# A clear of a small unused tile on GpSimd behind every gather from a table in HBM

## The chip, the core and the metric

The kernel runs on one core of a Trainium2 chip. The metric is the device time of one execution in microseconds (us): the median of several runs. A core has five engines that each work through an instruction stream of their own: TensorE (PE in the profile), VectorE (DVE), ScalarE (ACT), GpSimd (POOL) and SyncE (SP). They wait for one another by semaphores only. DMA transfers are issued by SP, ACT or POOL and run beside the engines.

## What is computed

One message-passing layer of a graph network, with a residual and a layer norm. There are 12,500 nodes with 128 features (x) and 400,000 edges, sorted by destination, each with a length. Cut to what matters, with the constants left out:

```python
rbf = exp(-(d[:, None] - centers) ** 2 / (2 * width ** 2))          # 50 per edge
cut = 0.5 * (cos(pi * d / 10) + 1) * (d <= 10)
W = (silu(rbf @ fw1 + fb1) @ fw2 + fb2) * cut[:, None]              # 128 per edge
messages = (x[src] @ pw + pb) * W
agg = segment_sum(messages, dst, 12500)
out = layernorm(2 * x + silu(agg @ mw1 + mb1) @ mw2 + mb2)
```

Edges longer than 10 contribute nothing. The kernel drops them first and works on those that are left.

## The kernel before

**Tiles and stages.** The edges that are left are handled in 139 quads (`NL`) of 512 edges: four groups of 128, one edge to a partition. Instead of multiplying each gathered row of x by `pw`, the kernel multiplies all 12,500 rows once in the first 60 us or so (`project`) and stores the products in HBM as the table of products, `proj`. From there on a quad needs only its rows of `proj`. For the first 12 quads (`FROM_X`), which come before that table is there, rows of x are gathered and multiplied afterwards (`multiply`, line 983).

**One quad.** `radial` loads the lengths, `basis` makes the radial functions (ACT), `first`, `silu` and `second` are the two layers that give W (PE, ACT, PE). `message` (line 1103) multiplies W with the gathered rows on DVE at line 1110; `place` (line 1117) makes one-hot matrices on DVE at line 1122, which hold the destination and the cutoff; `sum_up` (line 1134) multiplies messages and one-hot matrices on PE, and `add` (line 1161) adds the sums into the node table `aggT` on DVE. Node layers and layer norms of finished nodes are worked in between (`nodes`) and the last of them at the end (`tail` and the lines behind the loop).

**Packing.** Which edges are left, in which order, is worked out on the chip in seven chunks (`pack_first`, `pack`, `unpack`), mostly on DVE. Each chunk sends its list to HBM with one indirect DMA from POOL (line 487) and reads it back; that gives the indices `srci` (line 891) by which rows are gathered.

**The gathers.** `fetch` (line 1026) issues one indirect DMA on POOL for each group of 128 edges: 128 rows of 512 bytes, to one quarter of a buffer. In the first 12 quads the table is x; from quad 12 on it is `proj`. In eight quads (`SINGLY`) the first group is not gathered but loaded row by row from SP (`one_by_one`). That makes 48 gathers from x and 500 from `proj`. The rare branches behind the main path (`more`, `everything`), which these inputs don't take, call `fetch` with an `idx` of their own.

**What sets the order.** The schedule is written out by hand (`tc.manual_schedule()`): each engine executes its instructions in the order in which the Python code emits them. `fetches` (line 435) decides when a gather is emitted. It keeps a model of POOL's time, `pool[0]`, which grows by 1.29 us with each gather, and emits gathers up to a given time or quad. POOL's own stream holds nothing but the gathers of line 1032, the seven scatters of line 487 and a few small instructions in the first 5 us, so on POOL their order is fixed, and the model decides only how the seven scatters stand among the gathers, and how the instructions of other engines stand to each other. Buffers (`quad_sb`, 21 of them) come free when the message that used them is done; a gather into a used buffer waits for that. POOL has no other work.

Of the kernel before, what the change touches and what calls it, by code (L numbers as in the profile page):

```python
# [10 lines left out]
F32 = mybir.dt.float32  # L11
# [9 lines left out]
P = 128  # L21
# [5 lines left out]
WIDE_0 = 128  # L27
WIDTHS = (56, 56, 80, 112, 80, 104, 128)
QT = 4
QE = QT * P  # L30
WS = 500
SB = 14
# [48 lines left out]
def kernel(  # L81
# [37 lines left out]
    nc = tc.nc  # L119
# [4 lines left out]
    NP = 2 * NQ  # L124
    MW = 2 * (NQ * QE + QE)

    CLEAR = (0, 128 * P, 384 * P, MW)
    assert H == P == W and DIRECT % QT == 0 and LISTS <= 5
    assert E == P * sum(ROWS) and E % P == 0 and W <= N <= 1 << SB
# [4 lines left out]
    keep = ctx.enter_context(tc.tile_pool(name="keep", bufs=1))  # L134
# [54 lines left out]
    make_identity(nc, ident)  # L189
    quad_sb = [keep.tile([P, QT, H], F32, name=f"quad{k}") for k in range(GOT)]  # L190
    x4_sb = [keep.tile([P, QT, H], F32, name=f"x4{k}") for k in range(X_BUFS)]
    quad_sb += x4_sb
# [62 lines left out]

    ones_b = keep.tile([96, QE], BF16, name="ones_b")
    nc.vector.memset(ones_b, 1.0)
# [34 lines left out]
    def ends():  # L292


        nc.vector.tensor_scalar(end, part_f, 2.0, float(2 * NQ * QE - FIRST_W),
                                op0=OP.mult, op1=OP.add)
# [108 lines left out]
    def place_of(q):  # L405
        n, later = LATER
        while len(placed) <= q:
            k = len(placed)
            last = {}
            for m, b in enumerate(placed):  # L410
                last[b] = m
            allowed = range(len(quad_sb)) if k < n else later
            cap = max(4, min(20, 20 - (k - 30) // 4))
            ok = [b for b in allowed if last.get(b, -99) <= k - cap]
            never = [b for b in allowed if b not in last]
            if k < len(quad_sb):
                placed.append(k)
            elif ok:
                placed.append(max(ok, key=lambda b: last.get(b, -99)))
            else:  # L420
                placed.append(min(allowed, key=lambda b: last.get(b, -99)))
        return placed[q]
# [12 lines left out]
    def fetches(until, most):  # L435

        while fetched[0] < QT * min(most, known[0]) and pool[0] <= until:
            q, j = divmod(fetched[0], QT)
            fetch(q, table=x if q < FROM_X else None, js=(j,))
            if j == 0:  # L440
                pool[0] = max(pool[0], summed.get(before_it(q), 0.0))
            if j or q not in SINGLY:
                pool[0] += 1.29
            there_at[q] = pool[0] + 2.2
            fetched[0] += 1
# [349 lines left out]
    def unpack(c):  # L795
# [8 lines left out]
        def listed(t, a, b, l0, l1):  # L804
            (nc.scalar if c < 1 else nc.sync).dma_start(t[a:b, :l1 - l0],
                              packed[l0:l1, (p0 + a) * 512:(p0 + b) * 512]
                              .rearrange("s (p w) -> p s w", w=512))
# [3 lines left out]
        if c < 2:  # L811
            more_ = np_ if c == 0 else SPILL
            also = work.tile([P, 2, QE], F32, name="s", bufs=3).bitcast(I32)
            listed(also, 0, more_, 3, LISTS)
# [194 lines left out]
    def one_by_one():  # L1009

        row_at[0] = max(row_at[0], clock[0] - 8.0)
        while singles and row_at[0] < clock[0]:
# [4 lines left out]
            if e % AT_ONCE == 0:  # L1017
# [5 lines left out]
                              proj.rearrange("n f -> (n f)").bitcast(U8)[ds(rows_at[e % AT_ONCE], 4 * H)]  # L1023
                              .rearrange("(o f) -> o f", o=1))

    def fetch(q, idx=None, table=None, js=range(QT)):
        got = quad_sb[place_of(q) if q >= 0 else 0]
        for j in js:
            if q in SINGLY and j == 0:
                continue  # L1030
            i = srci[:, 2 * q + j // 2, j % 2:j % 2 + 1] if idx is None else idx[:, j:j + 1]
            nc.gpsimd.indirect_dma_start(  # L1032
                out=got[:, j, :], out_offset=None, in_=proj if table is None else table,
                in_offset=bass.IndirectOffsetOnAxis(ap=i, axis=0))
        got_of[q] = got

    def quads(o):
# [3 lines left out]
    def radial(o, lengths):  # L1041

        n = math.prod(lengths.shape) // QE
        d = work.tile([P, QE], F32, name="d", bufs=3)
        v = lengths.rearrange("(o h) e -> o h e", o=1)
# [494 lines left out]
    def more(q):  # L1540

        fetch(-2, srci[:, 2 * q:2 * q + 2, :].rearrange("p r j -> p (r j)"))
        radial(-1, near_d[2 * q:2 * q + 2].rearrange("(o p) e -> o (p e)", o=1))
        basis(-1)
        first(-1)
        silu(-1)
        second(-2)
        pu_of[q], got_of[q] = pu_of.pop(-2), got_of.pop(-2)
        place(q)
        msg = message(q)  # L1550
        pa_of["two"] = ps.tile([P, 2, 2 * W], F32, name="sums", bufs=2)
        sum_up(q, msg)
        base_of(q)
        add(q)

    def everything():
        nc.vector.memset(aggT, 0.0)
        def again(e0, seen):
# [18 lines left out]
            cosine(wgt)  # L1577
            nc.vector.scalar_tensor_tensor(wgt, wgt, 1.0, near, op0=OP.add, op1=OP.mult)
            fetch(-2, idx)
            radial(-1, edge_weight[ds(e0, QE)].rearrange("(o e) -> o e", o=1))  # L1580
            basis(-1)
# [65 lines left out]
```

## Time and profile before

| | |
|---|---|
| time, median of 3 runs | 727.36 us (726.96 to 729.21) |
| time of the profiled execution | 731.18 us |
| its span, first to last instruction | 729.3 us |
| mean granted TensorE clock | 0.926 |
| gathers from `proj` (line 1032) | 421 into `quad` buffers, 79 into `x` buffers |
| gathers from x (line 1032) | 48 |
| scatters (line 487) | 7 |

How to read the profile: a row of the groups has the line, the engine, the operation, output and inputs by name, and a count; then the busy time in us and the mean of one in ns; then the idle time of the engine just ahead of these instructions and what ended it. A row of the timeline begins with the start and the length in us and ends, in brackets, with the idle time ahead. "issue" is idle time that ended by nothing that the profile shows. A row of the waits has the total in us, the number of waits and the longest. In the rows of one line's summary stand the shortest, median and longest duration in ns and the first and last start. POOLq and DVEq are the sequencers of POOL and DVE.

### The profile page before, as it was taken

Reading aid. Unit: us, or ns where it says so; the run is one execution under the profiler, and the core shown is the slowest. Engines: PE = TensorE matmul, PEld = TensorE weight load, DVE = VectorE, ACT = ScalarE, POOL = GpSimd, SP = SyncE. Lnnn points to the kernel's source line nnn. Section 1 sums busy time; section 2 is a strip of 40 time slices with the busy share of each in tenths; the row PEclk is TensorE's granted clock in tenths of the full one; section 3 lists DMA queues with packets and bytes.
Section 4 is the critical chain, followed back from the end, with each engine's and each line's share of the span. In section 5 each row is a group of like instructions: output and inputs, shape, how many; then the busy total and the mean of one; then the engine's idle time right before and its main releaser. Section 6 shows DMA issues by size and latency. Waiting matters only on the chain.

```text
span 729.3 us, 13631 instructions
## 1 busy us (share of the span) xinstructions
PE 591.7 (81%) x3531; PEld 463.5 (64%) x3531; DVE 561.8 (77%) x1734; ACT 402.7 (55%) x572; POOL 532.4 (73%) x569
## 2 busy tenths in 40 slices
PE   6878777797888797888788979999977878887974
PEld 5767566576656676667466757777755656565752
DVE  8897998878968998989689959768555546564774
ACT  6547634275345864536347364839644744374584
POOL 6776777777777777777777777777777777777770
PEclk9998887999989998999889998999998989999998
DMA  8995443243234333242333343434433433445242
GB/s 262 326 314 182 124 134 87 68 145 90 87 100 140 86 96 106 84 141 81 88 99 121 104 105 114 147 116 142 126 99 113 139 99 98 112 125 149 55 139 69
DMA packets 53104, 91.38 MB, mean 125 GB/s; under 512 B 13824, under 2 KB 20576, under 8 KB 53018
## 3 DMA queue, kind: packets, MB, share of 16 engines
q1 hardware_dynamic: 34610, 53.34, 22.0%
q0 software_dynamic: 17840, 36.77, 19.6%
q8 instruction: 30, 0.49, 0.3%
q14 instruction: 56, 0.46, 0.2%
q10 hardware_dynamic: 568, 0.33, 0.2%
HBM read 74.59 MB, written 15.79 MB: 124 GB/s over the span
## 4 chain that ended last, share of the span: by engine, by line
DVE 25%; POOL 18%; PE 17%; issue 16%; DMA 15%; ACT 4%; DVEq 2%; SPq 1%; POOLq 0%; ACTq 0%
POOL quad L1032 14%; DMA quad<-proj,srci 7%; POOL x L1032 5%; DVE hot L1122 4%; PE bank L1099 4%; PE sums L1142 4%; PE ph L1082 3%; DVE aggT L1165 2%; DVE msg L1110 2%; PE bank L327 2%; DMA pair<-packed 2%; DVEq L1151 2%; DMA proj<-hp 2%; DVE r_d L502 2%; DVE quad L1122 2%
## 5 line engine op out<-in xcount | busy, mean ns | idle before, releaser
L1032 POOL DMA_INDIRECT quad<-proj,srci x421 | 400.5, 951 | 130.5 <-issue 104.9
L1099 PEld LDWEIGHTS bank<-fw_sb,s 128*128 128x128 f32 x1112 | 162.2, 210 | 67.5 <-issue 60.0
L1088 ACT ACTIVATE s<-ph 128x1024 f32<-128x1024 f32 x70 | 71.2, 1017 | 169.9 <-PE ph L1082 169.8
L1099 PE MATMUL bank<-fw_sb,s 128*128 128x128 f32 x1112 | 162.1, 293 | 0.0
L1082 PE MATMUL ph<-rbf,w_sb 102*128 102x512 f32 x278 | 141.1, 632 | 9.2 <-ACT rbf L1074 4.9
L1142 PEld LDWEIGHTS sums<-hot,msg 128*128 128x128 f32 x816 | 106.4, 196 | 55.2 <-DVE msg L1110 27.1
L1122 DVE TENSOR_SCALAR hot<-iota_n,dl,cut 128x80 f32<-128x80 f32 (+4 forms) x408 | 108.7, 343 | 24.8 <-PE sums L1142 22.0
L1142 PE MATMUL sums<-hot,msg 128*128 128x80 f32 (+4 forms) x816 | 109.5, 278 | 14.2 <-DVE msg L1110 13.9
L1096 PE MATMUL bank<-fb_b,ones_b 96*128 96x512 bf16 x139 | 56.8, 409 | 49.0 <-DVE msg L1110 24.5
L1032 POOL DMA_INDIRECT x<-proj,srci x79 | 75.3, 953 | 24.1 <-issue 20.7
L1110 DVE TENSOR_TENSOR msg<-bank,quad 128x512 f32<-128x512 f32 (+1 forms) x82 | 55.4, 676 | 41.6 <-DMA quad<-proj,srci 30.8
L1082 PEld LDWEIGHTS ph<-rbf,w_sb 102*128 102x128 f32 x278 | 50.5, 202 | 47.4 <-issue 36.7
L1165 DVE TENSOR_TENSOR aggT<-aggT,sums 128x80 f32 (+4 forms) x209 | 53.7, 257 | 27.4 <-PE sums L1142 10.7
L1073 ACT ACTIVATE rbf<-d,rbf_bias,rbf_scale 102x512 f32<-102x512 f32 x70 | 56.2, 803 | 26.5 <-DMA d<-near_d 26.4
L1032 POOL DMA_INDIRECT quad<-in_x_dram,srci x48 | 47.0, 979 | 18.7 <-issue 14.7
L327 PEld LDWEIGHTS bank<-pw_sb,xT 128*128 128x128 f32 (+1 forms) x292 | 43.5, 215 | 11.3 <-ACT xT L968 5.0
L1088 ACT ACT_TABLE_LOAD x36 | 46.2, 1283 | 0.6
L1074 ACT ACT_TABLE_LOAD x35 | 44.9, 1283 | 0.6
L327 PE MATMUL bank<-pw_sb,xT 128*128 128x128 f32 (+1 forms) x292 | 44.5, 301 | 0.8 <-ACT xT L968 0.6
L1074 ACT ACTIVATE rbf<-rbf 102x512 f32<-102x512 f32 x70 | 44.1, 630 | 1.5
L1142 PE MATMUL sums<-quad,quad 128*128 128x128 f32 (+3 forms) x296 | 42.4, 290 | 2.2 <-DVE quad L1110 1.9
L1110 DVE TENSOR_TENSOR quad<-bank,quad 128x512 f32<-128x512 f32 (+2 forms) x40 | 25.1, 631 | 24.3 <-DMA quad<-proj,srci 20.4
(268 smaller groups left out, 809.9 us busy)
## 6 DMA issues: line engine op xcount, KB each, us to landing
d<-near_d SPq DMA_DIRECT2D x70, 256.0 KB
dl<-proj SPq DMA_DIRECT2D x1024, 0.5 KB
x<-in_x_dram SPq DMA_DIRECT2D x46, 256.0 KB
quad<-proj,srci POOLq DMA_INDIRECT x421
proj<-hp SPq DMA_DIRECT2D x24, 256.0 KB
out_dram<-x SPq DMA_DIRECT2D x22, 256.0 KB
r_d<-in_edge_weight_dram SPq DMA_DIRECT2D x5, 256.0 KB
r_dst<-in_dst_dram SPq DMA_DIRECT2D x5, 256.0 KB
```

The lines of the kernel that those rows point to most:

```text
L327: nc.tensor.matmul(to[:m, k, :], lT[:, k * P:k * P + m], w, start=False, stop=(k == a + c - 1))
L1032: nc.gpsimd.indirect_dma_start(out=got[:, j, :], out_offset=None, in_=proj if table is None else table, in_offset=bass.IndirectOffsetOnAxi ...
L1073: nc.scalar.activation(rbf[:u], d[:u], AF.Square, bias=rbf_bias[:u], scale=rbf_scale[:u])
L1074: nc.scalar.activation(rbf[:u], rbf[:u], AF.Exp, scale=-1.0 / (2.0 * width * width))
L1082: nc.tensor.matmul(ph[:, h, :], w1_sb[:2 * KR, h, :], rbf[:2 * KR], start=True, stop=True)
L1088: nc.scalar.activation(s[:, :n], ph[:, :n], AF.Silu)
L1096: nc.tensor.matmul(pu, ones_b[:, :P], bias_b["fb2"].rearrange("k j f -> k (j f)"), start=True, stop=False)
L1099: nc.tensor.matmul(pu[:, j * H:(j + 1) * H], s[:, j * P:(j + 1) * P], fw2_sb, start=False, stop=(j == QT - 1))
L1110: nc.vector.tensor_mul(msg[:, a:b, :], pu_of[q].rearrange("p (j f) -> p j f", j=QT)[:, a:b, :], got_of[q][:, a:b, :])
L1122: nc.vector.tensor_scalar(hot[:, j, :wide(q)], iota_n[:, :wide(q)], dl[:, at[0], at[1]], cut[:, at[0], at[1]], op0=OP.is_equal, op1=OP.mult)
L1142: nc.tensor.matmul(pa[:, k * W:k * W + wide(q)], msg[:, j, :], hot[:, j, :wide(q)], start=(j % n == 0), stop=(j % n == n - 1))
L1165: nc.vector.tensor_add(to, to, pa[:, k * W:k * W + wide(q)])
```

## The change

A tile `pause` of 128 partitions by 128 float32 is added. Behind each gather from `proj` on the main path, GpSimd sets it to zero. No instruction reads the tile. The gathers from x and those of the rare branches get no clear. The model of POOL's time in `fetches` stays as it was.

```diff
@@ -27,6 +27,7 @@
 QT = 4
+PAUSE = 128
 QE = QT * P
@@ -1023,6 +1024,8 @@
+    pause = keep.tile([P, PAUSE], F32, name="pause")
+
     def fetch(q, idx=None, table=None, js=range(QT)):
         got = quad_sb[place_of(q) if q >= 0 else 0]
         for j in js:
@@ -1032,6 +1035,8 @@
             nc.gpsimd.indirect_dma_start(
                 out=got[:, j, :], out_offset=None, in_=proj if table is None else table,
                 in_offset=bass.IndirectOffsetOnAxis(ap=i, axis=0))
+            if table is None and idx is None:
+                nc.gpsimd.memset(pause, 0.0)
         got_of[q] = got
```

## The prediction

> **What bounds the kernel now.** I read the page first: the busy shares, the slices, the groups.
>
> ```profile
> span 729.3 us, 13631 instructions
> PE 591.7 (81%) x3531; PEld 463.5 (64%) x3531; DVE 561.8 (77%) x1734; ACT 402.7 (55%) x572; POOL 532.4 (73%) x569
> POOL 6776777777777777777777777777777777777770
> L1032 POOL DMA_INDIRECT quad<-proj,srci x421 | 400.5, 951 | 130.5 <-issue 104.9
> L1032 POOL DMA_INDIRECT x<-proj,srci x79 | 75.3, 953 | 24.1 <-issue 20.7
> L1032 POOL DMA_INDIRECT quad<-in_x_dram,srci x48 | 47.0, 979 | 18.7 <-issue 14.7
> ```
>
> By busy share PE and DVE look more loaded than POOL. The slices say otherwise: POOL stands at 7 from the second slice to the last but one, and never varies. An engine with slack would show dips. The groups say what the missing three tenths are: 421 + 79 = 500 gathers from the table of products have 130.5 + 24.1 = 154.6 us of idle time ahead of them, 0.31 us each, most of it put down to "issue", that is, to no other engine. Next I read POOL's timeline, a piece from the middle and the end, and the one line's own summary.
>
> ```profile
> 73.87 0.94 POOL L1032 DMA_INDIRECT quad<-proj,srci  x1 [0.30 <-issue]
> ...
> 299.66 0.94 POOL L1032 DMA_INDIRECT quad<-proj,srci  x1 [0.30 <-issue]
> 300.91 0.94 POOL L1032 DMA_INDIRECT quad<-proj,srci  x1 [0.30 <-issue]
> 302.16 0.99 POOL L1032 DMA_INDIRECT quad<-proj,srci  x1 [0.30 <-issue]
> ...
> 709.49 0.94 POOL L1032 DMA_INDIRECT quad<-proj,srci  x1 [0.30 <-issue]
> L1032 POOL DMA_INDIRECT quad<-proj,srci x421: 938/944/1344, 73.9 to 709.5; - x141
> ```
>
> A gather starts every 1.25 us, 0.94 busy and 0.30 idle, from 73.87 to 709.49. That is 635.6 us; 500 gathers at 1.25 make 625, and the scatters of line 487 that stand between them nearly all the rest. So POOL never truly waits: its chain of gathers runs end to end for 87% of the span. The waits of the other engines confirm who follows whom.
>
> ```profile
> DVE msg L1110 <- DMA quad<-proj,srci: 30.8, 15, 4.1
> DVE quad L1110 <- DMA quad<-proj,srci: 20.4, 13, 2.5
> ```
>
> These rows of the waits, from 500 us to the end, give the whole of the 51.2 us that DVE's multiplication waited for gathers; before 500 us it waited for none. Consumers start with a store of fetched quads, use it up, and from 500 us on follow the gathers. POOL is what ends last.
>
> **The change, part by part.** It adds one instruction, a memset of 128x128 f32 on POOL behind each of the 500 gathers; the 48 gathers from x get none. Nothing is removed or moved. The tile is read by nobody, so no instruction waits for a memset; a memset can only wait for the one before it, over a microsecond old. What counts is what it does to POOL's 1.25 us. What is queued behind it is the next gather, and behind all gathers their consumer, the multiplication of line 1110, and the scatters of line 487. As POOL has no slack, a delay d per gather costs 500 x d.
>
> Is there cover in the 0.30 us of idle time? The trace has one gather with no gather ahead of it:
>
> ```profile
> 6.65 0.16 DVE L539 TENSOR_SCALAR srci<-most_f 128x8 int32<-128x8 int32 x1
> 7.11 1.21 POOL L1032 DMA_INDIRECT quad<-in_x_dram,srci  x1 [2.41 <-DVE srci L539]
> 8.62 0.94 POOL L1032 DMA_INDIRECT quad<-in_x_dram,srci  x1 [0.30 <-issue]
> ...
> L1032 POOLq EVENT_SEMAPHORE  x1: 17/17/17, 113.8 to 113.8; - x1
> 113.24 0.94 POOL L1032 DMA_INDIRECT x<-proj,srci  x1 [0.30 <-issue]
> ```
>
> Its index was written at 6.65 + 0.16 = 6.81 and it starts at 7.11, the same 0.30 us later, though POOL had been idle for over 2 us. So the 0.30 is a lead that each gather brings along from the moment that it is free to go, not time in which the engine lies fallow. Nor is it the sequencer's time: that handled a wait at 113.8, in the middle of the gather of 113.24 to 114.18, so it already works on later instructions while a gather runs, and a memset's own issue is hidden there. I therefore put the memset wholly beside the lead, not into it: no cover.
>
> What does the memset occupy? POOL's start-up rows:
>
> ```profile
> 0.26 0.10 POOL L1635 MEMSET const-float32-0.0<- 128x1 f32 x1 [0.26 <-issue]
> 0.29 0.10 POOL L1635 MEMSET const-float32-1.0<- 128x1 f32 x1
> ...
> 0.74 0.20 POOL masks.py:197 MEMSET ident<- 128x128 f32 x1 [0.29 <-POOLq L1635]
> 1.02 0.29 POOL masks.py:199 TENSOR_SCALAR_AFFINE_SELECT ident<-ident 128x128 f32<-128x128 f32 x1
> 1.28 0.55 POOL L194 IOTA quad<- 128x500 int32 x1
> 1.79 0.12 POOL L196 IOTA part_i<- 128x1 int32 x1
> masks.py:197 POOL MEMSET ident<- 128x128 f32 x1 | 0.2, 204 | 0.3 <-POOLq L1635 0.3
> ```
>
> The same operation at the same size is there once: 204 ns. A memset of one column lasts 100 ns, but the next one starts 30 ns later, so 70 ns of its row overlap its successor. The lower bound is hence 30 + (204 - 100) = 134 ns: the spacing for one column and the 104 ns for 127 more. The row itself, 204 ns, is the upper bound where nothing overlaps. An independent successor does overlap a little: the second iota starts at 1.79, while the first runs to 1.28 + 0.55 = 1.83. I take the middle, 0.169 us, as an estimate between the two; it is what this overlap leaves too (0.204 - 0.04). 500 x 0.169 = **+84.5 us** (67 to 102). Below nothing is excluded by the single gather above, unless the rival D holds.
>
> The Trainium skill's Perfetto Trace Analysis, section "GPSIMD Engine Instruction", says that a GpSimd span is not to be trusted and that the spacing from start to start is to be taken. Taken literally it gives 1.02 - 0.74 for this memset and the sum of rival B; but the successor there reads the tile that the memset writes, which no gather here does, so the trace leaves it open.
>
> What the delay absorbs: of POOL's 154.6 us of idle time, 500 x 0.30 are leads; 4.6 are real waits, and two rows name them.
>
> ```profile
> POOL quad L1032 <- DVE at_row L905: 1.7, 1, 1.7
> POOL quad L1032 <- DVE quad L1110: 1.1, 1, 1.1
> 714.38 0.29 DVE L1110 TENSOR_TENSOR quad<-bank,quad 128x128 f32<-128x128 f32 x1 [0.76 <-issue]
> ```
>
> A later POOL need not wait there: 1.4 + 0.8 us beyond the lead, say 2. The last gather ends at 709.49 + 0.94 = 710.43, its product is multiplied only at 714.38, behind other work of DVE. With consumers that wait for each gather that work is done earlier: another 2 us. No new wait of POOL arises, as what it waits for depends on earlier gathers and on unchanged work; the later scatters of line 487 shift with POOL by the same rule.
>
> Sum, against the profiled execution: 731.18 us (span 729.3 and 1.9 around it) + 84.5 - 4 = 811.7. The median of the runs shown, 727.36, lies 3.8 below the profiled one; the forecast for the median is 727.4 + 84.5 - 4 = **808 us**, with a range of its own of 790 (134 ns) to 825 (204 ns).
>
> **The rivals.**
>
> A, hidden: the 0.30 us is a pause of the engine and 0.204 fits into it. For: it is called idle time. Against: the single gather's 0.30. Time 727 us, same as before; if half of the forecast's price is hidden, 765.
>
> B, dear: the gather starts only when the memset is fully through, and pays an ordinary gap besides. The spacing 1.02 - 0.74 = 0.28 shows that for a dependent successor. 727.4 + 140 - 4 = 863 us. Against: nothing depends on the memset.
>
> C, cold: a gather behind another kind of operation starts up anew. The first gather of all lasted 1.21 where 0.944 is the median: 0.27 more. 0.169 + 0.27 = 0.44 us, 727.4 + 220 - 4 = 943 us. Against: the one after it, 8.62, is back at 0.94, but none of the trace's gathers has a memset ahead of it.
>
> E, port: a memset and VectorE's operations from SBUF to SBUF shut each other out.
>
> ```profile
> L1122 DVE TENSOR_SCALAR hot<-iota_n,dl,cut 128x80 f32<-128x80 f32 (+4 forms) x408 | 108.7, 343 | 24.8 <-PE sums L1142 22.0
> ```
>
> They fill 108.7 of 635.6 us, 17%; a memset that meets one waits half of 343 ns on average: 0.17 x 0.17 = 0.03 us, 500 times 15 us, 823 us. Against: the gathers run beside the same operations and their mean, 951, is only 7 ns above the median. The Trainium skill's SBUF — State Buffer, section "Who interferes with whom", has the rule: whichever of VectorE in a two-port mode and GpSimd comes first holds the shared ports for its whole instruction. By that rule it would be 823, and the trace does not bear it out for gathers.
>
> D, faster: the 0.30 is charged only where a gather follows a gather, and the memset breaks that. Then a memset after an ordinary gap of 0.08 (1.02 - 0.74 - 0.20), 0.204 long, with the gather on its heels as the iota is (-0.04), makes 0.244 in place of 0.30: -0.056 x 500 = -28, 699 us. It decides from the point where gap, memset and gap together stay under 0.30. Against: the single gather again, which follows no gather and has its 0.30. That the memset isn't issued at all I leave out: it is an instruction like the start-up memsets, which have their rows.
>
> **How the numbers follow.** Forecast 0.50; E 0.09; B 0.22; C 0.07; A 0.10 (0.06 wholly hidden, 0.04 in part); D 0.02. The range holds forecast, E and B and is opened a little beyond B and below 790 for a partial cover: 770 to 875, leaving out C, D and most of A, 0.19 in all. A measurement of this kernel can tell 0.3%, some 2.2 us, from no change. Faster: D, 0.02. Same: A wholly hidden, 0.06. Slower: the rest, 0.92.
>
> **What would show it.** In the changed kernel's timeline each gather from the table should be followed by a MEMSET row, and gathers should start 1.39 to 1.45 us apart; the groups should have 500 memsets near 0.2 us. The lead ahead of a gather, counted from the memset's end, should stay near 0.30. If it shrinks to 0.1 with the spacing at 1.25, A holds; a spacing of 1.53 is B, gathers of 1.2 us are C, memsets well over 0.2 us beside VectorE's operations are E, a spacing under 1.25 is D. POOL's last gather should end near 793, with some 17 us behind it; DVE's waits for gathers should start well before 500 us and sum to over 100 us. The forecast is wrong above all if a memset behind a gather costs something that the start-up rows, with no gather near, cannot show.

## The result, and the profile after

The changed kernel takes 776.52 us (median of 4 runs, 775.47 to 776.91), the kernel before, run beside it, 728.29 us (726.96 to 730.58). The ratio is 1.063, with a 95% interval of 1.060 to 1.067. The two profiled executions took 776.13 and 731.18 us.

The page after, span, POOL's slices and the groups of the gathers and clears. The gather is now line 1035, the clear line 1039.

```profile
span 774.4 us, 14131 instructions
POOL 6778888878888887888888888888888888888881
L1035 POOL DMA_INDIRECT quad<-proj,srci x421 | 404.5, 961 | 74.3 <-issue 66.2
L1039 POOL MEMSET pause<- 128x128 f32 x500 | 113.4, 227 | 0.3
L1035 POOL DMA_INDIRECT x<-proj,srci x79 | 75.7, 958 | 13.4 <-issue 12.9
```

There are 500 clears with rows of 227 ns, 113.4 us in all. But the idle time ahead of the gathers fell from 130.5 + 24.1 = 154.6 to 74.3 + 13.4 = 87.7 us, by 66.9. So more than half of the clears' busy time came out of time that POOL had shown as idle. POOL's timeline after, near the end, shows how:

```profile
740.14 0.95 POOL L1035 DMA_INDIRECT quad<-proj,srci  x1 [0.17 <-issue]
741.08 0.23 POOL L1039 MEMSET pause<- 128x128 f32 x1
741.48 0.95 POOL L1035 DMA_INDIRECT quad<-proj,srci  x1 [0.17 <-DVE dif L1210]
742.43 0.22 POOL L1039 MEMSET pause<- 128x128 f32 x1
742.81 0.95 POOL L1035 DMA_INDIRECT quad<-proj,srci  x1 [0.17 <-issue]
...
756.35 0.95 POOL L1035 DMA_INDIRECT quad<-proj,srci  x1 [0.17 <-DVE rs L1219]
```

The clear's row begins where the gather's row ends, and the idle time ahead of the next gather is 0.17 us where it was 0.30. Gathers start some 1.335 us apart (the median over the trace; 1.249 before): +0.086 us. 500 x 0.086 = 43 us, nearly the whole result.

The balance of the profiled executions: the first gather from the table starts at 71.5 (73.87 before), -2.4; from there to the start of the last, at 756.35, it takes 684.8 us (635.6), +49.2; behind that 18.0 us are left (19.8), -1.8. Together +45.0 us, as measured between these two executions. The -2.4 is not the clears' doing, as none has run by then; other kernels with clears start their gathers at up to 74.6. Of the 49.2 the spacing makes 43; about 4.5 come from five places at which POOL stands still although no row names a reason that holds at all of them; the rest, 1.7, is what is left of smaller lengthenings and of two waits that are gone. The first of the five places:

```profile
155.98 0.95 POOL L1035 DMA_INDIRECT quad<-proj,srci  x1 [0.17 <-issue]
156.93 0.22 POOL L1039 MEMSET pause<- 128x128 f32 x1
159.18 0.96 POOL L1035 DMA_INDIRECT quad<-proj,srci  x1 [2.03 <-PE sums L1147]
```

2.03 in place of 0.17 there, the same again at 303.5, and 0.42 to 0.45 in place of 0.17 at 447.3, 590.3 and 733.4: always 106 indirect DMAs apart, gathers and scatters counted together. The waits of DVE after, longest of their kind:

```profile
DVE msg L1115 <- DMA quad<-proj,srci: 48.8, 19, 5.0
DVE quad L1115 <- DMA quad<-proj,srci: 30.4, 17, 4.3
DVE two L824 <- DMA pair<-packed: 24.8, 3, 11.8
DVE two L824 <- DMA dl<-proj: 11.5, 1, 11.5
```

DVE waits 79.2 us for gathers (51.2 before), still none of it before 500 us. The last two rows suggest why: before 500 us it is now held up by something else that comes from POOL, the read-back of the chunks' lists, whose scatters stand among the gathers. Line 824 reads nothing but these lists, also where the row names another transfer as the last to land; its waits are 36.3 us (7.5 + 6.0 before).

### The profile page after: what moved, and what is told of

The parts are those of the page before. It is cut to its first block, busy times and chain, and to the rows that moved or that the text cites. A ratio compares the mean times of both kernels' runs of the same rounds, so it can differ in the third digit from the quotient of the medians.

```text
span 774.4 us, 14131 instructions
## 1 busy us (share of the span) xinstructions
PE 596.9 (77%) x3531; PEld 465.7 (60%) x3531; DVE 563.4 (73%) x1734; ACT 402.5 (52%) x572; POOL 649.3 (84%) x1069
## 4 chain that ended last, share of the span: by engine, by line
POOL 27%; DVE 9%; PE 8%; DMA 6%; issue 5%; DVEq 1%; ACT 0%; POOLq 0%; SPq 0%
POOL quad L1035 22%; POOL pause L1039 5%; DMA quad<-proj,srci 5%; PE ph L1087 2%; PE bank L1104 2%; PE sums L1147 2%; DVE hot L1127 1%; DVE aggT L1170 1%; DVE quad L1127 1%; DVE msg L1115 1%; DMA pair<-packed 1%; DVEq L1156 1%; PE bank L328 1%; PE bank L1179 1%; DVE quad L1115 1%
## 5 line engine op out<-in xcount | busy, mean ns | idle before, releaser
L1035 POOL DMA_INDIRECT quad<-proj,srci x421 | 404.5, 961 | 74.3 <-issue 66.2
L1087 PE MATMUL ph<-rbf,w_sb 102*128 102x512 f32 x278 | 143.6, 642 | 7.4 <-ACT rbf L1079 3.9
L1147 PE MATMUL sums<-hot,msg 128*128 128x80 f32 (+4 forms) x816 | 111.8, 282 | 28.9 <-DVE msg L1115 28.7
L1039 POOL MEMSET pause<- 128x128 f32 x500 | 113.4, 227 | 0.3
L1035 POOL DMA_INDIRECT x<-proj,srci x79 | 75.7, 958 | 13.4 <-issue 12.9
L328 PEld LDWEIGHTS bank<-pw_sb,xT 128*128 128x128 f32 (+1 forms) x292 | 41.4, 206 | 11.0 <-ACT xT L969 5.1
```

What stands on the lines that cost most here:

```text
L1035: nc.gpsimd.indirect_dma_start(out=got[:, j, :], out_offset=None, in_=proj if table is None else table, in_offset=bass.IndirectOffsetOnAxi ...
L1039: nc.gpsimd.memset(pause, 0.0)
L1087: nc.tensor.matmul(ph[:, h, :], w1_sb[:2 * KR, h, :], rbf[:2 * KR], start=True, stop=True)
L1147: nc.tensor.matmul(pa[:, k * W:k * W + wide(q)], msg[:, j, :], hot[:, j, :wide(q)], start=(j % n == 0), stop=(j % n == n - 1))
```

## The experiments

Theory 1 after the result: POOL's chain is the bound, and part of what a clear needs is covered once per gather. Rivals: a clear is just cheap and nothing is covered (theory 2); it costs by what it does to the transfers, not by POOL's time. A second question is what the five stalls are.

**w1, w512: the size of the clear.** `PAUSE = 128` becomes 1 and 512.

> The changed kernel with a clear of one column (128x1) behind each of the 500 gathers in place of 128 columns. In the changed kernel a clear has a row of 0.218 us, the idle time ahead of a gather falls from 0.30 to 0.17, and gathers start 1.335 us apart in place of 1.25: +0.085 us. Theory 1, cover: about 0.13 us of whatever stands between two gathers fits into the 0.30 us ahead of a gather and costs nothing; the row of a one-column clear is 0.10 us, so it is hidden whole: spacing 1.25 us, time 728 us, as before. Theory 2, serial: nothing is hidden, the clear just occupies GpSimd for less than its row, 0.03 us to start it and some 0.055 us for the other 127 columns: spacing 1.28 us, 728 + 500 x 0.03 = 743 us.

> A clear of 512 columns behind each gather. Theory 1, cover: beyond what is hidden each further column costs the 0.82 ns that the rows of the start-up clears give (104 ns for 127 columns): 0.085 + 384 x 0.00082 = 0.40 us, spacing 1.65 us, time 728 + 200 = 928 us. Theory 2, serial: a column costs 0.055 / 127 = 0.43 ns: 0.085 + 384 x 0.00043 = 0.25 us, spacing 1.50 us, time 853 us.

w1: 733.81 us against 729.38, ratio 1.0056 (1.0017 to 1.0095). w512: 932.81 us. POOL's timeline of w1, then of w512:

```profile
400.06 0.12 POOL L1039 MEMSET pause<- 128x1 f32 x1
400.37 0.95 POOL L1035 DMA_INDIRECT quad<-proj,srci  x1 [0.19 <-issue]
401.31 0.12 POOL L1039 MEMSET pause<- 128x1 f32 x1
401.62 0.94 POOL L1035 DMA_INDIRECT quad<-proj,srci  x1 [0.19 <-DVE quad L1127]
```

```profile
402.06 0.95 POOL L1035 DMA_INDIRECT quad<-proj,srci  x1 [0.17 <-issue]
403.01 0.54 POOL L1039 MEMSET pause<- 128x512 f32 x1
403.71 0.95 POOL L1035 DMA_INDIRECT quad<-proj,srci  x1 [0.17 <-issue]
```

With one column the gathers start 1.249 us apart, as without any clear, although a row of 0.12 us now stands between them. With 512 columns the spacing is 1.655 us. From 128 to 512 columns it grows by 0.320 us, 0.83 ns a column, the rate of the start-up rows (0.82). Theory 1 gave 1.25 and 1.65, theory 2 gave 1.28 and 1.50. Theory 2 is out. The time follows the spacing: 729.4 + 500 x 0.406 = 932.4, measured 932.8. Only the 4 us of w1 are not explained by it; cols, below, ties them to the five stalls.

**w32: where the cost begins.** `PAUSE = 32`.

> A clear of 32 columns behind each gather. Theory 1, cover: the line through 128 and 512 columns meets 1.249 us at 25 columns, so 32 columns cost about 6 ns: spacing 1.255 us, 731 us. Theory 3, a step: the cost is not a line with a covered beginning, but one column is a special case (nothing to loop over), and 32 columns lie on a line between 1 and 128 columns: 31 x 0.68 ns = 21 ns, spacing 1.270 us, 739 us.

This run, with two, ring4 and last_only, was made on a chip on which the kernel before itself took 1085 us: in w32, ring4 and last_only engines stood still for up to 31 us at a time, for what the trace calls remote (below, the largest such row of w32's DVE waits), and gathers waited for their consumers. So from these four runs only the spacing in stretches without such waits is read.

```profile
DVE hot L1127 <- remote: 123.1, 15, 16.0
```

```profile
434.64 0.95 POOL L1035 DMA_INDIRECT x<-proj,srci  x1 [0.17 <-issue]
435.60 0.14 POOL L1039 MEMSET pause<- 128x32 f32 x1
435.90 0.95 POOL L1035 DMA_INDIRECT x<-proj,srci  x1 [0.17 <-issue]
```

The median spacing is 1.258 us, nearer to theory 1's 1.255 than to 1.27. On the same chip the gathers of last_only that have no clear ahead of them are 1.253 apart (1.249 on the other chip), so the clear costs some 5 ns, as theory 1 has it, and not 21. The time of 1099.02 us against 1085.06 says nothing on the clear.

**two, two_sep: a second clear, which has no gather ahead of it.** First with one tile (two), where the line `nc.gpsimd.memset(pause, 0.0)` stands twice; then with two tiles (two_sep):

```diff
-                nc.gpsimd.memset(pause, 0.0)
+                nc.gpsimd.memset(pauses[0], 0.0)
+                nc.gpsimd.memset(pauses[1], 0.0)
```

> Two clears of 128 columns behind each gather. The runs so far: a clear of 1 column leaves the spacing of the gathers at 1.249 us, 128 columns make it 1.335, 512 columns 1.655, that is 0.83 ns for each column beyond the first 26 or so. Theory 1, cover: a clear occupies GpSimd for 0.03 + 127 x 0.00083 = 0.135 us, as the start-up rows say, and some 0.05 us of it fits into the 0.30 us ahead of a gather; the second clear finds no cover and costs the whole 0.135: spacing 1.47 us, 728 + 500 x 0.22 = 838 us. Theory 2, cheap clear: a clear costs 0.086 us wherever it stands: spacing 1.42 us, 728 + 500 x 0.172 = 814 us.

> Two clears of 128 columns behind each gather, to two different tiles, so that the second waits for nothing recent. With one tile for both the second clear began only 0.06 us behind the end of the first, as it waits for it, and added 0.25 us to the spacing. Theory 1, cover: a clear occupies GpSimd for 0.03 + 127 x 0.00083 = 0.135 us and some 0.05 us are covered once per gather: spacing 1.335 + 0.135 = 1.47 us. Theory 2, cheap clear: 1.335 + 0.086 = 1.42 us.

With one tile (two) both forecasts missed: some 300 of 494 gathers start about 1.585 us behind the last, and another 133 start 1.95 behind it, with an idle time of 0.52 us where the others have 0.16, which stays unexplained. The second clear writes what the first wrote and so waits for its end, as the affine select of the start-up does for the clear before it. Timeline of two, then of two_sep:

```profile
403.22 0.22 POOL L1039 MEMSET pause<- 128x128 f32 x1
403.50 0.20 POOL L1040 MEMSET pause<- 128x128 f32 x1
403.86 0.95 POOL L1035 DMA_INDIRECT x<-proj,srci  x1 [0.16 <-issue]
```

```profile
402.99 0.23 POOL L1039 MEMSET pause<- 128x128 f32 x1
403.14 0.23 POOL L1040 MEMSET pause<- 128x128 f32 x1
403.53 0.95 POOL L1035 DMA_INDIRECT quad<-proj,srci  x1 [0.16 <-issue]
404.48 0.22 POOL L1039 MEMSET pause<- 128x128 f32 x1
404.62 0.22 POOL L1040 MEMSET pause<- 128x128 f32 x1
405.00 0.95 POOL L1035 DMA_INDIRECT quad<-proj,srci  x1 [0.16 <-issue]
```

With two tiles the second clear starts 0.14 to 0.15 us behind the first, over the first's row, and the spacing is 1.475 us: the second clear costs 0.140 us, theory 1's 0.135 and not 0.086. So a clear of 128 columns occupies POOL for 0.14 us, and behind a gather 0.054 of it are covered. The time, 854.69 us, is 11 us more than 730.7 + 500 x 0.226 = 843.7. In POOL's chain they are there: 3.9 us at the same five places as above, the rest in gathers that start 0.1 to 0.3 us late, for which no row names a reason. The 998.86 us of two, below the kernel before on that chip, stay unexplained; its gathers hardly waited for consumers, unlike those of w32.

**lo64, hi64: which half of the partitions.** `memset(pause[:64], 0.0)` and `memset(pause[64:], 0.0)`.

> The clear takes partitions 0 to 63 only, 128 columns each. It is to tell apart where the time is spent. Theory 1a, the engine as a whole takes one instruction after the other: the same as the changed kernel, spacing 1.335 us, 776 us, here and with the other half. Theory 1b, each of GpSimd's cores works on its own partitions and only those that also make the gather's descriptors count: the same as the changed kernel here and less with the other half. By the Trainium skill's Perfetto Trace Analysis, section on the SWDGE instruction, those are the first two cores, which own low partitions.

> The clear takes partitions 64 to 127 only. Theory 1a, the engine as a whole: spacing 1.335 us, 776 us. Theory 1b, only the cores that make the descriptors count, and they have no column to clear here: between no cost and that of a one-column clear, spacing 1.25 to 1.28 us, 728 to 743 us.

776.19 and 776.47 us. Timelines of lo64, then hi64:

```profile
400.19 0.95 POOL L1035 DMA_INDIRECT quad<-proj,srci  x1 [0.17 <-issue]
401.14 0.22 POOL L1039 MEMSET pause<- 64x128 f32 x1
401.53 0.95 POOL L1035 DMA_INDIRECT quad<-proj,srci  x1 [0.17 <-issue]
```

```profile
399.47 0.95 POOL L1035 DMA_INDIRECT quad<-proj,srci  x1 [0.16 <-issue]
400.43 0.22 POOL L1039 MEMSET pause<- 64x128 f32 x1
400.81 0.95 POOL L1035 DMA_INDIRECT quad<-proj,srci  x1 [0.16 <-issue]
```

Either half costs as much as the whole, 1.335 us, as theory 1a has it. The Trainium skill's GPSIMD Engine Reference, section 2.1, says that each core goes on to the next instruction as soon as it is done with its own partitions. No gain from that shows here; whether the cores without a partition go through the same loop can't be seen.

**cols, ring4b: the five stalls.** In cols each clear takes another column of the tile, so no clear waits for another; in ring4b the clear goes to four tiles in turn.

```diff
-                nc.gpsimd.memset(pause, 0.0)
+                nc.gpsimd.memset(pause[:, fetched[0]:fetched[0] + 1], 0.0)   # cols, with PAUSE = 560
+                nc.gpsimd.memset(pauses[fetched[0] % 4], 0.0)                # ring4, ring4b
```

> A clear of one column behind each gather, each time another column of the tile, so that no clear waits for an earlier one. With one and the same column the spacing was 1.249 us as before, yet the time was 0.2 to 1.0% above the kernel before, and GpSimd stood still 1.9 us ahead of two gathers and 0.3 to 0.5 us ahead of three. Theory L1, lookahead: the clear's wait keeps the sequencer from running ahead, and fresh instructions come too late; without the wait the stalls go and the time is that of the kernel before, ratio 1.000. Theory L2, longer stream: the stalls come with 500 more instructions, wait or not: ratio 1.005.

> The clear of 128 columns goes to four tiles in turn, so that a clear waits for the one four gathers back and not for the last one. In the changed kernel GpSimd stands still for 1.9 us ahead of two gathers (at 159 and 303 us), and for 0.3 us ahead of three later ones, at equal distances of some 240 to 250 instructions of GpSimd's stream, in all kernels with clears, however long; the kernel before has none. Theory L1, lookahead: fresh instructions are being fetched there, and the sequencer, held up by the clear that waits for the last clear, is only one gather ahead, too little to cover it; with four tiles it is further ahead, the two long stalls vanish or shrink, and 3 to 4.5 us go: 772 to 773 us, at a spacing of 1.335 us as before. Theory L2, longer stream: the stalls come with the doubled number of instructions alone: 776 us.

> The kernel of the four tiles in turn once more, on another chip, since the kernel before itself took 1085 us on the last one. Theory L1, lookahead: the clear waits for the one four gathers back, the sequencer gets further ahead, the two stalls of 1.9 us shrink: ratio to the kernel before 1.058 to 1.060. Theory L2, longer stream: 1.063 to 1.065 as with one tile.

cols: 730.65 us against 730.73, ratio 0.998 (0.996 to 1.001), where w1, with the same 500 clears of one column, had 1.0056. The same gather in w1, then in cols:

```profile
152.60 0.94 POOL L1035 DMA_INDIRECT quad<-proj,srci  x1 [0.19 <-issue]
153.54 0.16 POOL L1039 MEMSET pause<- 128x1 f32 x1
155.77 0.95 POOL L1035 DMA_INDIRECT quad<-proj,srci  x1 [2.07 <-DVE bank L509]
```

```profile
152.20 0.94 POOL L1035 DMA_INDIRECT quad<-proj,srci  x1 [0.19 <-issue]
153.13 0.17 POOL L1039 MEMSET pause<- 128x1 f32 x1
153.45 0.95 POOL L1035 DMA_INDIRECT quad<-proj,srci  x1
```

ring4b: 772.94 us, ratio 1.0564 (1.0523 to 1.0605), 4 us less than 1.0634 would give (777.1). Its spacing is 1.335 us as in the changed kernel, and the same gather starts on time:

```profile
157.97 0.95 POOL L1035 DMA_INDIRECT quad<-proj,srci  x1 [0.17 <-PE sums L1147]
158.91 0.23 POOL L1039 MEMSET pause<- 128x128 f32 x1
159.30 0.96 POOL L1035 DMA_INDIRECT quad<-proj,srci  x1 [0.17 <-issue]
```

All five stalls are gone in both. Theory L1 holds as far as it says that the wait of a clear for the last clear causes them: the stream is as long in cols and ring4b as in w1 and the changed kernel. The intervals of ring4b and the changed kernel overlap a little, but the stalls are gone from every place in its trace.

That the wait holds the sequencer back can be read too. POOL's sequencer handles 156 semaphore waits of the gathers' line in each kernel; the more it is ahead, the earlier the last of them comes. The rows of the kernel before, the changed one and cols, in this order:

```profile
L1032 POOLq EVENT_SEMAPHORE  x156: 17/17/8555, 12.9 to 698.5; - x156
L1035 POOLq EVENT_SEMAPHORE  x156: 17/17/2767, 11.9 to 750.9; - x156
L1035 POOLq EVENT_SEMAPHORE  x156: 17/17/6310, 12.2 to 699.4; - x156
```

The last gathers start at 709.5, 756.3 and 710.5. So the last wait is handled some 9 spacings ahead of the last gather in the kernel before and in cols, and 4 in the changed kernel; it is 4 in w1, two_sep and w512 too, and 7 in ring4b. The size of the stalls fits: at the first two places 3.16 to 3.20 us pass from the start of one gather to that of the next in w1, the changed kernel, two_sep and w512 alike, though their spacings run from 1.249 to 1.655; at the other three it is 1.59 to 1.76, and w512, whose spacing is as long, has no stall there. This looks like something of a fixed length that one spacing covers in these kernels and the longer lead covers whole in cols and ring4b.

What that something is stays open. That instructions are being fetched was argued from equal distances in the stream, and two_sep speaks against it: with 500 instructions more than the changed kernel it has its stalls ahead of the same gathers. The distance is one of 106 indirect DMAs and not of so many instructions. On the disturbed chip ring4 took 1059.7 us against 1085.06, ratio 0.980 (0.968 to 0.992), which isn't read either way.

**last_only, last_only_b: fewer clears.** `if table is None and idx is None and j == QT - 1:`

> The clear of 128 columns stands only behind the fourth gather of each quad from the thirteenth on, 127 clears in place of 500. If the time is just GpSimd's chain: 127 x 0.086 = 10.9 us, 728 + 11 = 739 us, with a spacing of 1.335 us behind those gathers and 1.249 us behind the others. If the clears cost by spacing the transfers (less overlap of the gathers in flight) and not by their own time, less: near 728 us.

> The kernel with 127 clears once more, on another chip. If the time is GpSimd's chain alone: 127 x 0.086 = 11 us above the kernel before, some 739 us. If the clears cost by spacing the transfers: near the kernel before.

On the disturbed chip 1072.79 against 1085.06 us. On the other 743.88 against 730.73 us: +13.2. 127 x 0.086 make 10.9 (its gathers are 1.328 us apart where a clear stands between them, 1.251 elsewhere); the rest is about what one wait of last_only_b has grown by:

```profile
POOL quad L1035 <- DVE at_row L906: 4.2, 1, 4.2
```

It was 1.7 us before. There is one run of this kernel on each chip; the price goes with the number of clears, so it is POOL's time and not the transfers' order.

On the undisturbed chip no version was faster than the kernel before; cols comes out level with it.

## Why the prediction was right, and what it mis-sized

**That POOL's chain of gathers is the bound** held throughout: in w512, last_only_b and the changed kernel the time follows the gathers' spacing, from 0.09 to 0.41 us per gather. Three readings on the way to it were loose. POOL's slices do vary: the fourth is 6, from a stretch ahead of the first gather from the table. Of the 12 us by which the chain exceeds its spacings, the five scatters make 6.5, about half and not nearly all. And the lead is 0.305 us rather than 0.30, so that 2.1 us and not 4.6 were real waits, which the two rows named account for whole.

**The number came out within the range in part by luck.** The rise was forecast as 80.5 us and was 48.2. The measured 776.5 lies outside the 790 to 825 that the forecast's own terms allow, and inside 770 to 875 only because the range was opened below for a partial cover, an outcome that the prediction gave 0.04 and counted among what the range leaves out (its 0.19 takes in all of A). And 4.5 us of stalls that it did not foresee came on top, about as much as the 4 us that it took off.

**The price of a clear**, the main term, was 0.169 us and measured 0.086, so +84.5 us became +43. Two steps of it were off. The clear's own time was taken as the middle between 0.134 and 0.204; two_sep has 0.140, so the bound from the spacing of the start-up clears was right and the row was not. The Trainium skill's Perfetto Trace Analysis, section "GPSIMD Engine Instruction", has that rule, spacing before span, and the trace agrees if one takes the spacing to a successor that doesn't depend on it. And "no cover" failed: 0.054 us are covered; by 0.03 us and 0.83 ns a further column that is an estimated 25 to 30 columns. The argument was one gather that starts 0.30 us behind its index with an idle engine. It shows that the lead belongs to the gather, not that POOL can do nothing else in it. Where in the 0.30 the cover lies, ahead of the gather or at the end of the last one, stays open.

**"A memset can only wait for the one before it, over a microsecond old"** was true of the clear itself and overlooked what the wait does to the sequencer: it is some 5 gathers less ahead, which brings 4.5 us of stalls that are gone in ring4b and cols.

**What the delay absorbs**, 4 us, came about in the rows: the two waits named are gone, and 1.8 us fewer stand behind the last gather, though that is one execution of each kernel. But DVE's waits for gathers, forecast well before 500 us and above 100 us, were 79.2 us and none before 500: it seems that the lists' read-back held DVE up first, an effect that the forecast had put down as shifting with POOL and had not followed to DVE.

**The rivals.** A, hidden, was partly right: it is what w1 and cols show for one column, and its half-hidden price, 765, is the nearest to 776.5. B, the dear clear, is what two shows for a dependent successor: 0.25 us. C, a cold gather, fell: gathers behind a clear last 0.950 where 0.944 was the median. D fell: no run has a median spacing under 1.249. E, the ports, asks for clears that meet DVE's operations and last longer; their rows run from 218 to a median of 219 and a mean of 227 ns, 8 ns or 4 us in all at most.

## What to carry to other kernels

Idle time ahead of an engine's rows that comes back in equal pieces is neither free room nor wholly taken: put a small instruction of two sizes into it and read the spacing from start to start. The time that a short instruction takes of a saturated engine is its spacing to an independent successor (0.140 us here), which its row overstates (0.22); what is covered comes off that, and only a run with the instruction in its place shows how much (0.054). And let a repeated write go to several tiles in turn, since a wait on the last such instruction, though met by the time it counts, keeps the sequencer from running ahead.

## What the runs showed of the hardware that was not expected

- A clear of one column between two gathers adds nothing to their spacing of 1.249 us, though its row is 0.12 us long.
- A clear of 64 partitions costs GpSimd as much as one of 128, in either half: 1.335 us.
- A wait of each clear for the last one shortens the sequencer's lead from some 9 spacings to 4, as read at its last wait, and brings stalls of 1.9 us (two) and 0.3 to 0.5 us (three), always 106 indirect DMAs apart; without such waits they are gone.
- An independent clear starts 0.14 us behind another of 128 columns, 0.08 us ahead of that one's end; a dependent one 0.06 us behind its end.
